# Attention and routed experts on one core: the further tile and its branch ahead of the last expert's down product, two experts' weights in dead tiles, rows fetched on ACT's queue

## The chip, the cores and the metric

The kernel runs on one core of a Trainium2 chip. Its engines are TensorE (PE, with the weight loads shown apart as PEld), VectorE (DVE), ScalarE (ACT), GpSimd (POOL) and SyncE (SP). Each works through its own instructions in the order in which the program gives them. SP, ACT and POOL can start DMA transfers. The metric is the device time of one execution in microseconds (us).

## The reference

A transformer layer with the norms behind the additions: attention with 16 query and 4 key heads, then a layer norm, then eight routed experts of which each token takes one, plus a shared expert, then a second layer norm. All data are 32-bit floats: 2 x 1024 tokens of width 256, experts of inner width 512.

```python
x = L0_attn_x                                             # (2, 1024, 256)
x = _layernorm(x + attn(x, Wq, Wk, Wv, Wo))               # causal, ALiBi, 16 heads, 4 KV heads

logits = x @ router_w.T                                   # 8 experts
top_vals, top_idx = jax.lax.top_k(logits, 1)
scores = sigmoid(where chosen: top_vals, else -inf)
xr = x[None] * scores.T[:, :, None]
gate, up = split(einsum('eth,ehf->etf', xr, gate_up_proj))
routed = einsum('etf,efh->eth', up * silu(gate), down_proj)
shared = (silu(x @ shared_gate_w) * (x @ shared_up_w)) @ shared_down_w
x = _layernorm(x + shared + routed.sum(axis=0))
```

## The kernel before

The program has two stages. The first (lines 262 to 919) does attention for all 16 tiles of 128 tokens, the first norm, the routing, and the shared expert for three of its four blocks of 512 tokens. The second (from line 928) does the rest. The change lies in the second stage. The order of all five engines' work there is the order of the program text (a manual schedule), and waits between engines and DMAs follow from what each instruction reads and writes.

**Slots.** Each expert owns two tiles of 128 slots in the DRAM tensor `slot_x` (`OWN = 2`). A token's row (its 256 numbers, its number `NUM` and its weight `WT`) is scattered to a slot by POOL with an indirect DMA (`scatter_x`, line 250). Tokens beyond an expert's 256 slots go to further tiles, which are made of four quarters of 32 slots, each quarter of one expert (`QU = 4`). `place_more` (line 957) computes the places of these tokens and, for each quarter, the expert it belongs to (`more_e`); the 16 scatters with these second places (`slots2`) follow it, spread over several rounds of the loop. The first further tile is always computed; up to 13 more lie in a conditional block that runs only when more than four quarters are in use.

**One expert.** The steps, each a function of its own, are:

- `load` (940): gate and up weights `wgu` (1 MB) and down weights `wd` (0.5 MB), both on SP's queue. `wgu` has four buffers, `wd` five.
- `fetch` (1079): the expert's rows from `slot_x`, on SP's queue, into one of four `row` buffers.
- `weigh` (1099): DVE multiplies rows by their weights.
- `turn` (1105): TensorE transposes the rows, ACT copies them to `slot_xT`.
- `gate_and_up` (1133): 16 matmuls, which stand in the profile as 32 (each as two), in four groups of eight; two Silu on ACT (1150), two products `slot_h` on DVE (1151). The PSUM tiles of gate and up have two buffers each.
- `down_and_norm` (1154): for each of the two tiles the down product (1158, eight matmuls in the profile), then `norm_and_store` (1114): DVE adds to `zt` (1119), takes statistics (`layernorm`, 224), POOL raises to the power -0.5 (232), DVE normalizes (233), POOL scatters the rows to the output (238).
- `gather_z` (1084): POOL gathers into `zt` what the token has so far (input plus shared expert) from the DRAM tensor `z_dram`.
- For a further tile: `gate_and_up_more` (1171), `turn_h` (1190), `down_and_norm_more` (1198), with the weights of its quarters from `weights_of` (1214), which reads the expert's number at run time.

**The order.** The second stage first loads three experts, does the shared expert for the fourth block (`shared`, `shared_down`; its four results go to `z_dram` on SP's queue at line 1076), fetches rows 0 and 1 and loads expert 3. Then comes the loop over the experts (1236). Round e holds, in this order: the fetch of rows e + 2; the weighting of rows e + 1; gate and up of e; the load of e + 4; one quarter's weights in rounds 1 to 4; the turn of e + 1; down and norm of e - 1; the gathering of z for e + 1; in round 0 `place_more`; two to four of the second scatters. Behind the loop stand the further tile's gate and up, then the last expert's down and norm, then the further tile's down and norm, and at the very end the conditional block: every engine reads the number of quarters in use (line 1269) and branches (line 1275).

Of the kernel before, what the change touches and what calls it, by code (L numbers as in the profile page):

```python
# [9 lines left out]
F32 = mybir.dt.float32  # L10
# [6 lines left out]
P = 128  # L17
# [28 lines left out]
def attn_moe_postln_kernel(  # L46
# [15 lines left out]
    nc = tc.nc  # L62
    B, T, C = x.shape
    E, _, F2 = gate_up.shape
    FF = F2 // 2
    KC = C // P
# [861 lines left out]
    with (  # L928
# [8 lines left out]
        tc.tile_pool(name="rt2", bufs=1) as rtp,  # L937
        tc.manual_schedule(engines=MANUAL),
    ):
        def load(e, tag="", bufs=4):  # L940
            gu = wgup.tile([P, KC, F2], F32, tag=f"wgu{tag}", name="wgu", bufs=bufs)
            d = wgup.tile([P, FC, C], F32, tag=f"wd{tag}", name="wd", bufs=bufs + (bufs > 1))
            if isinstance(e, int):
                e = slice(e, e + 1)
            nc.sync.dma_start(out=gu, in_=gate_up[e].rearrange("e (c p) f -> p (e c) f", p=P))
            nc.sync.dma_start(out=d, in_=down[e].rearrange("e (c p) n -> p (e c) n", p=P))
            return gu, d
# [114 lines left out]
        def shared_down(tb, h):  # L1062
            for i in range(TPB):
                dp = ps_d.tile([P, C], F32, tag="d", name="dp")
                for f in range(FC):
                    nc.tensor.matmul(  # L1066
                        dp,
                        lhsT=h[:, f, ts(i, P)],
                        rhs=sh_d[:, f, :],
                        start=(f == 0),  # L1070
                        stop=(f == FC - 1),
                    )
                tt = tb * TPB + i
                z = actp.tile([P, C], F32, tag="z", name="z")
                nc.vector.tensor_add(z, xs[:, tt, :C], dp)
                nc.sync.dma_start(out=z_dram[ts(tt, P), :], in_=z)


        def fetch(first, n):
            row = slp.tile([P, n, ROW], F32, tag="row", name="row")  # L1080
            nc.sync.dma_start(out=row, in_=slot_xt[:, first : first + n])
            return row

        def gather_z(k, row, n):
            z = zts[k % 4]
            for i in range(n):
                nc.gpsimd.indirect_dma_start(
                    out=z[:, i],
                    out_offset=None,
                    in_=z_dram,  # L1090
                    in_offset=bass.IndirectOffsetOnAxis(
                        ap=row[:, i, NUM : NUM + 1].bitcast(I32), axis=0
                    ),
                    bounds_check=NTT * P - 1,
                    oob_is_err=False,
                )
            return z

        def weigh(row, n):
            for i in range(n):  # L1100
                nc.vector.tensor_scalar_mul(
                    row[:, i, :C], row[:, i, :C], row[:, i, WT : WT + 1]
                )

        def turn(row, n):
            tp = ps_t.tile([P, KC, n, P], F32, tag="t", name="xtp")
            for i in range(n):
                for c in range(KC):
                    nc.tensor.transpose(tp[:, c, i, :], row[:, i, ts(c, P)], ident)
            xT = slp.tile([P, KC, n * P], F32, tag="xT", name="slot_xT", bufs=2)  # L1110
            nc.scalar.copy(xT, tp.rearrange("p c n q -> p c (n q)"))  # L1111
            return xT
# [20 lines left out]
        def gate_and_up(xT, e):  # L1133
            h = hp.tile([P, FC, OWN * P], F32, tag="h", name="slot_h")
            for f in range(0, FC, 2):
                gp = ps_gu.tile([P, 2, OWN * P], F32, tag="g", name="gp")
                up = ps_gu.tile([P, 2, OWN * P], F32, tag="u", name="up")
                for dst, off in ((gp, 0), (up, FF)):
                    for j in range(2):
                        for c in range(KC):  # L1140
                            col = off + (f + j) * P
                            nc.tensor.matmul(  # L1142
                                dst[:, j],
                                lhsT=ws[e][0][:, c, col : col + P],
                                rhs=xT[:, c, :],
                                start=(c == 0),
                                stop=(c == KC - 1),
                            )
                sg = actp.tile([P, 2, OWN * P], F32, tag="sg", name="sg")
                nc.scalar.activation(sg, gp, AF.Silu)  # L1150
                nc.vector.tensor_mul(h[:, f : f + 2], sg, up)
            return h

        def down_and_norm(row, z, h, e):
            def dps(i):
                dp = ps_d.tile([P, C], F32, tag="d", name="dp")
                for f in range(FC):
                    nc.tensor.matmul(  # L1158
                        dp,
                        lhsT=h[:, f, ts(i, P)],  # L1160
                        rhs=ws[e][1][:, f, :],
                        start=(f == 0),
                        stop=(f == FC - 1),
                    )
                return dp

            norm_and_store(row, z, OWN, dps)
# [30 lines left out]
        def down_and_norm_more(row, z, hT, ws):  # L1198
            def dps(i):
                dp = ps_d.tile([P, C], F32, tag="d", name="dp")  # L1200
                for f in range(FC):
                    for k, (_, d_q) in enumerate(ws):
                        nc.tensor.matmul(
                            dp[ts(k, QP)],
                            lhsT=hT[:, f, ts(k, QP)],
                            rhs=d_q[:, f, :],
                            start=(f == 0),
                            stop=(f == FC - 1),
                        )
                return dp  # L1210

            norm_and_store(row, z, 1, dps)

        def weights_of(j, k):

            e = nc.values_load(
                more_e[0:1, j * QU + k : j * QU + k + 1],
                engines=(mybir.EngineType.SP,),
                min_val=0,
                max_val=E - 1,  # L1220
                skip_runtime_bounds_check_because="a count of at most E, bounded by E - 1",
            )
            return load(bass.ds(e, 1), f"{k}", 1)


        ws = {e: load(e) for e in range(3)}
        h = shared(2)
        rows = {e: fetch(e * OWN, OWN) for e in range(2)}
        ws[3] = load(3)
        shared_down(2, h)  # L1230
        weigh(rows[0], OWN)
        zs = {0: gather_z(0, rows[0], OWN)}
        xTs, hTs = {0: turn(rows[0], OWN)}, {}
        again = list(range(NTT))
        quarters = []
        for e in range(E):
            if e + 2 < E:
                rows[e + 2] = fetch((e + 2) * OWN, OWN)
            elif e + 2 == E:
                rows[E] = fetch(E * OWN, 1)  # L1240
            n = OWN if e + 1 < E else 1
            weigh(rows[e + 1], n)
            hTs[e] = gate_and_up(xTs.pop(e), e)
            if e + 4 < E:
                ws[e + 4] = load(e + 4)
            if 0 < e <= QU:
                quarters.append(weights_of(0, e - 1))
            xTs[e + 1] = turn(rows[e + 1], n)
            if e > 0:
                down_and_norm(rows.pop(e - 1), zs.pop(e - 1), hTs.pop(e - 1), e - 1)  # L1250
            zs[e + 1] = gather_z(e + 1, rows[e + 1], n)
            if e == 0:
                place_more()
            k = 4 if e == 0 else 3 if e < 3 else 2
            for tt in again[:k]:
                scatter_x(tt, slots2[:, tt : tt + 1])
            del again[:k]

        def more(k, row, z, xT, ws, before=()):
            h = gate_and_up_more(xT, ws)  # L1260
            for what in before:
                what()
            down_and_norm_more(row, z, turn_h(h), ws)

        def last_own():
            down_and_norm(rows[E - 1], zs[E - 1], hTs.pop(E - 1), E - 1)

        more(E, rows[E], zs[E], xTs.pop(E), quarters, [last_own])
        n = nc.values_load(
            how_many[0:1, 0:1],  # L1270
            min_val=0,
# [3 lines left out]
        with tc.If(n > QU):  # L1275
            for j in range(1, NO):
                quarters = [weights_of(j, k) for k in range(QU)]
                row = fetch(E * OWN + j, 1)
                weigh(row, 1)
                z = gather_z(E + j, row, 1)  # L1280
                more(E + j, row, z, turn(row, 1), quarters)


# [42 lines left out]
```

## Time and profile before

| what | us |
|---|---|
| median of 3 runs (lowest, highest) | 565.85 (565.15, 569.23) |
| the profiled execution, its own time | 567.34 |
| its span, from the first to the last instruction | 565.6 |
| TensorE busy | 538.3 (95% of the span) |
| VectorE busy | 340.0 |
| ScalarE busy | 261.8 |
| GpSimd busy | 153.1 |
| second stage, from about | 430 |

The profile is of one execution. Its page gives the busy time of each engine, the chain of work that ended last, groups of equal instructions with what ended the engine's idle time before them, and the DMA issues with their time to landing. The letter q behind an engine's name (SPq, PEldq, POOLq) marks its sequencer, which waits, branches and issues DMAs; such instructions are not counted as busy time. L1142 is line 1142 of the kernel. `out<-in` gives the tiles that an instruction writes and reads; x8 is a number of instructions. In a row of the time line the first two numbers are the start and the duration, and what ended the idle time before an instruction stands in brackets.

### The profile page before, as it was taken

To read this page: it belongs to the slowest core of one execution; us is meant where nothing else is said; L and a number is where in the kernel's file an instruction comes from. 1 tells how busy PE (TensorE), PEld (TensorE's weight loads), DVE (VectorE), ACT (ScalarE), POOL (GpSimd) and SP (SyncE) were. 2 spreads that over 40 slices of the span, in tenths; PEclk is the share of its full clock that TensorE was granted. 3 is DMA by queue.
4 is the path that set the end of the run, shared out by engine and by line. 5 is a ranking of instruction groups with operands and counts; after the bars stand their busy time and mean duration, and the time that the engine had idled before them with its cause. 6 is when DMAs were issued, how large, how long until landed. Compare 5 with 4: busy or idle time off the path is not lost.

```text
span 565.6 us, 8688 instructions
## 1 busy us (share of the span) xinstructions
PE 538.3 (95%) x3274; PEld 294.5 (52%) x3274; DVE 340.0 (60%) x808; ACT 261.8 (46%) x500; POOL 153.1 (27%) x183
## 2 busy tenths in 40 slices
PE   8999999999999999999999999999999999989990
PEld 4654444543333444434335544544755678878860
DVE  2398977787786777786867864333453245434451
ACT  3432876657666765756586764565111022111110
POOL 5310422201110111020423020142102036756642
PEclk9999999999999999998999999999999999989996
DMA  6212760000000000000100000110138555887210
GB/s 204 41 31 36 222 209 2 2 0 1 2 1 1 1 1 1 2 0 2 48 28 1 1 1 2 37 39 0 39 104 302 177 175 190 298 298 224 84 40 24
DMA packets 27119, 40.61 MB, mean 72 GB/s; under 512 B 3598, under 2 KB 20916, under 8 KB 27072
## 3 DMA queue, kind: packets, MB, share of 16 engines
q1 hardware_dynamic: 23088, 33.27, 18.9%
q0 software_dynamic: 3168, 6.34, 3.3%
q8 instruction: 27, 0.44, 0.3%
q10 hardware_dynamic: 816, 0.39, 0.2%
q14 instruction: 20, 0.16, 0.1%
HBM read 27.70 MB, written 12.58 MB: 71 GB/s over the span
## 4 chain that ended last, share of the span: by engine, by line
PE 76%; issue 8%; DVE 6%; ACT 4%; POOL 2%; DMA 1%; POOLq 0%; ACTq 0%; DVEq 0%
PE t_ps L503 18%; PE s_ps L418 10%; PE yT L547 10%; PE dp L1158 5%; PE gp L1142 4%; PE up L1142 4%; PE gu_sh L706 3%; DVE past L437 3%; PE qpj L292 3%; PE dp_sh L726 2%; PE o_ps L592 2%; PE kpj L292 1%; PE gp L1050 1%; PE vpj L327 1%; PE dp L1066 1%
## 5 line engine op out<-in xcount | busy, mean ns | idle before, releaser
L418 PE MATMUL s_ps<-kT,qT 32*128 32x512 f32 (+2 forms) x896 | 185.2, 472 | 1.8 <-ACT diag L452 0.8
L437 DVE TENSOR_REDUCE past<-s_ps 128x1 f32<-128x512 f32 (+3 forms) x256 | 148.0, 617 | 59.0 <-PE s_ps L418 51.9
L503 PE MATMUL t_ps<-qS,kT 32*128 32x512 f32 x576 | 169.1, 640 | 0.3 <-ACT pD L525 0.3
L522 ACT ACTIVATE pT<-t_ps 128x512 f32<-128x512 f32 x224 | 121.4, 600 | 77.0 <-PE s_ps L418 50.8
L418 PEld LDWEIGHTS s_ps<-kT,qT 32*128 32x128 f32 x896 | 79.6, 185 | 16.7 <-DVE past L437 4.9
L503 PEld LDWEIGHTS t_ps<-qS,kT 32*128 32x128 f32 x576 | 52.3, 184 | 59.5 <-issue 31.2
L547 PE MATMUL yT<-pT,v 128*32 128x512 f32 x448 | 60.4, 611 | 0.0
L232 POOL TENSOR_TENSOR rstd<-rstd,neg_half 128x1 f32<-128x1 f32 x33 | 18.8, 571 | 148.5 <-DVE rstd L231 148.5
L527 POOL TENSOR_SCALAR_AFFINE_SELECT pD<-pD 128x1024 f32<-128x1024 f32 x32 | 34.8, 1094 | 77.7 <-ACT pD L525 77.5
L238 POOL DMA_INDIRECT slot_x<-xs,slots x32 | 32.3, 1008 | 43.8 <-DVE slots L687 28.1
L525 ACT COPY pD<-t_ps 128x512 f32<-128x512 f32 x64 | 34.4, 601 | 20.0 <-PE s_ps L418 14.6
L706 PE MATMUL gu_sh<-x1T,sh_gu 128*128 128x512 f32 x96 | 43.6, 597 | 0.0
L455 POOL TENSOR_SCALAR_AFFINE_SELECT diag<-diag 128x1024 f32<-128x1024 f32 x16 | 17.5, 1094 | 92.3 <-ACT diag L452 92.3
L467 DVE TENSOR_REDUCE past<-diag 128x4 f32<-128x512 f32 x64 | 41.9, 676 | 0.0
L1150 ACT ACTIVATE sg<-gp 128x512 f32<-128x512 f32 x16 | 9.6, 597 | 56.1 <-PE gp L1142 56.1
L539 ACT ACTIVATE pD<-pD 128x1024 f32<-128x1024 f32 x32 | 34.3, 1072 | 0.7 <-POOL pD L527 0.7
L452 ACT COPY diag<-s_ps 128x128 f32<-128x128 f32 (+2 forms) x64 | 23.9, 377 | 22.5 <-DVE past L437 19.9
L1142 PE MATMUL gp<-slot_xT,wgu 128*128 128x256 f32 x128 | 30.5, 381 | 1.2 <-ACT slot_xT L1111 1.2
L1158 PE MATMUL dp<-wd,slot_h 128*128 128x256 f32 x128 | 30.6, 395 | 0.0
L450 DVE TENSOR_TENSOR diag<-s_ps,causal 128x128 f32<-128x128 f32 (+2 forms) x64 | 26.4, 415 | 7.1 <-PE s_ps L418 6.9
L1142 PE MATMUL up<-slot_xT,wgu 128*128 128x256 f32 x128 | 30.2, 379 | 0.0
L547 PEld LDWEIGHTS yT<-pT,v 128*32 128x32 f32 x448 | 8.8, 108 | 35.2 <-issue 34.0
(171 smaller groups left out, 619.4 us busy)
## 6 DMA issues: line engine op xcount, KB each, us to landing
wgu<-_L_ffn_gate_up_proj_dram SPq DMA_DIRECT2D x12, 1024.0 KB, 7.8
wd<-in_L_ffn_down_proj_dram SPq DMA_DIRECT2D x12, 512.0 KB, 6.7
slot_x<-empty SPq DMA_DIRECT2D x1, 3900.0 KB, 17.8
row<-slot_x SPq DMA_DIRECT2D x8, 260.0 KB, 2.8
xs<-in_L_attn_x_dram SPq DMA_DIRECT2D x4, 512.0 KB, 6.8
qT<-q_all SPq DMA_DIRECT2D x32, 64.0 KB, 2.3
z_dram<-z_sh SPq DMA_DIRECT2D x12, 128.0 KB, 1.8
sh_gu<-L_ffn_shared_gate_w_dram SPq DMA_DIRECT2D x1, 512.0 KB, 3.9
```

The source lines that it names most:

```text
L418: lambda r=r: nc.tensor.matmul(sp[:, r * n * P : (r + 1) * n * P], lhsT=qT[b][rows, r0 + r, ts(qt, P)], rhs=kT[b][rows, key * P : (key + n ...
L437: nc.vector.tensor_reduce(past[:, h * HALF + j, heads, parts[b, qt][key]], sp[j][:, :, : past_n * P], AX.X, ALU.max, negate=True,)
L467: lambda g=g: nc.vector.tensor_reduce(past[:, g, :, 0], diag[:, g], AX.X, ALU.max, negate=True),
L503: lambda: nc.tensor.matmul(tp, lhsT=kT[b][rows, ts(kt, P)], rhs=qS[b, qt][rows].rearrange("p r q -> p (r q)"), start=True, stop=True,)
L522: nc.scalar.activation(p[:, j], tp[j], AF.Exp)
L525: nc.scalar.copy(p[:, j], tp[j])
L527: nc.gpsimd.affine_select(out=p, in_=p, pattern=[[0, HALF * REP], [1, P]], compare_op=ALU.is_ge, fill=MASKED, base=0, channel_multiplier=-1,)
L539: lambda: nc.scalar.activation(p, p, AF.Exp),
L547: nc.tensor.matmul(yTs[b, qt][g * PAD : (g + 1) * PAD], lhsT=vs[b][:, kt, g, :], rhs=p[:, g, :], start=start, stop=stop,)
L706: nc.tensor.matmul(gu[k], lhsT=sh_gu[:, c, col : col + P], rhs=x1T[:, c, ts(tb, TB)], start=(c == 0), stop=(c == KC - 1),)
L1142: nc.tensor.matmul(dst[:, j], lhsT=ws[e][0][:, c, col : col + P], rhs=xT[:, c, :], start=(c == 0), stop=(c == KC - 1),)
L1158: nc.tensor.matmul(dp, lhsT=h[:, f, ts(i, P)], rhs=ws[e][1][:, f, :], start=(f == 0), stop=(f == FC - 1),)
```

## The change

- **Rows on ACT's queue.** `fetch` issues on ACT's queue; only rows 0 and 1, which are fetched ahead of the loop, stay on SP's.
- **Dead tiles.** The weights of experts 4 and 5 are loaded ahead of `shared_down`, into tiles whose contents are no longer needed: gate and up into the two halves of `x1T`, down into the two halves of `sh_gu`. Loads 6 and 7 follow in rounds 0 and 1. `wd` has four buffers instead of five.
- **Order.** The list `works` puts the further tile (E) between experts 6 and 7 in the loop: its gate and up come where expert 7's were, and its down product follows expert 7's gate and up. The conditional block stands behind the loop, and the last expert's down and norm behind the conditional block.
- **Second scatters.** Rounds 1 to 4 issue three each (before: 3, 3, 2, 2, 2 in rounds 1 to 5).

```diff
-        def load(e, tag="", bufs=4):
-            gu = wgup.tile([P, KC, F2], F32, tag=f"wgu{tag}", name="wgu", bufs=bufs)
-            d = wgup.tile([P, FC, C], F32, tag=f"wd{tag}", name="wd", bufs=bufs + (bufs > 1))
+        def load(e, tag="", bufs=4, place=None):
+            if place is None:
+                gu = wgup.tile([P, KC, F2], F32, tag=f"wgu{tag}", name="wgu", bufs=bufs)
+                d = wgup.tile([P, FC, C], F32, tag=f"wd{tag}", name="wd", bufs=bufs)
+            else:
+                gu, d = place
...
-        def fetch(first, n):
-            row = slp.tile([P, n, ROW], F32, tag="row", name="row")
-            nc.sync.dma_start(out=row, in_=slot_xt[:, first : first + n])
+        def fetch(first, n, queue=nc.scalar, tag="row", bufs=4):
+
+            row = slp.tile([P, n, ROW], F32, tag=tag, name="row", bufs=bufs)
+            queue.dma_start(out=row, in_=slot_xt[:, first : first + n])
...
         ws = {e: load(e) for e in range(3)}
         h = shared(2)
-        rows = {e: fetch(e * OWN, OWN) for e in range(2)}
+        rows = {e: fetch(e * OWN, OWN, nc.sync) for e in range(2)}
         ws[3] = load(3)
+        for i in range(2):
+
+            d = sh_gu[:, i].rearrange("p (f c) -> p f c", f=FC)
+            ws[4 + i] = load(4 + i, place=(x1T[:, :, ts(i, F2)], d))
         shared_down(2, h)
+        works = [*range(E - 1), E, E - 1]
+        many = {w: OWN if w < E else 1 for w in works}
...
+        begin(0)
+        xTs[0] = turn(rows[0], OWN)
+        for i, w in enumerate(works):
+            if i + 2 < len(works):
+                v = works[i + 2]
+                rows[v] = fetch(v * OWN, many[v])
+            if i + 1 < len(works):
+                weigh(rows[works[i + 1]], many[works[i + 1]])
+            if w < E:
+                hTs[w] = gate_and_up(xTs[w], w)
+            else:
+                h = gate_and_up_more(xTs[w], quarters)
+            if i < 2:
+                ws[6 + i] = load(6 + i)
+            if 0 < i <= QU:
+                quarters.append(weights_of(0, i - 1))
+            if i + 1 < len(works):
+                xTs[works[i + 1]] = turn(rows[works[i + 1]], many[works[i + 1]])
+            if i > 0:
+                down_of(works[i - 1])
+            if w == E:
+                hTs[w] = turn_h(h)
+            if i + 1 < len(works):
+                begin(works[i + 1])
+            if i == 0:
                 place_more()
-            k = 4 if e == 0 else 3 if e < 3 else 2
+            k = 4 if i == 0 else 3
             for tt in again[:k]:
                 scatter_x(tt, slots2[:, tt : tt + 1])
             del again[:k]
...
         with tc.If(n > QU):
             for j in range(1, NO):
...
+        down_of(E - 1)
```

Here `begin(w)` gathers z for w, and `down_of(w)` is `down_and_norm` for an expert and `down_and_norm_more` for the further tile.

More of the change, by code (lines that the diff above doesn't have):

```diff
@@ L1076, in shared_down, with gather_z @@
                 nc.sync.dma_start(out=z_dram[ts(tt, P), :], in_=z)
-        def fetch(first, n):
-            row = slp.tile([P, n, ROW], F32, tag="row", name="row")
-            nc.sync.dma_start(out=row, in_=slot_xt[:, first : first + n])
-            return row
-        def gather_z(k, row, n):
-            z = zts[k % 4]
+        def fetch(first, n, queue=nc.scalar, tag="row", bufs=4):
+            row = slp.tile([P, n, ROW], F32, tag=tag, name="row", bufs=bufs)
+            queue.dma_start(out=row, in_=slot_xt[:, first : first + n])
+            return row
+        def gather_z(z, row, n):
             for i in range(n):
@@ L1227, in attn_moe_postln_kernel @@
         h = shared(2)
-        rows = {e: fetch(e * OWN, OWN) for e in range(2)}
+        rows = {e: fetch(e * OWN, OWN, nc.sync) for e in range(2)}
         ws[3] = load(3)
+        for i in range(2):
+            d = sh_gu[:, i].rearrange("p (f c) -> p f c", f=FC)
+            ws[4 + i] = load(4 + i, place=(x1T[:, :, ts(i, F2)], d))
         shared_down(2, h)
-        weigh(rows[0], OWN)
-        zs = {0: gather_z(0, rows[0], OWN)}
-        xTs, hTs = {0: turn(rows[0], OWN)}, {}
-        again = list(range(NTT))
@@ L1235, in attn_moe_postln_kernel @@
[L1235 to L1252, printed above, removed]
+        works = [*range(E - 1), E, E - 1]
@@ new lines, in attn_moe_postln_kernel, with begin, down_of @@
+        many = {w: OWN if w < E else 1 for w in works}
+        zs, xTs, hTs, quarters = {}, {}, {}, []
+        again = list(range(NTT))
+        def begin(w):
+            zs[w] = gather_z(zts[w % 4], rows[w], many[w])
+        def down_of(w):
+            if w < E:
+                down_and_norm(rows[w], zs[w], hTs[w], w)
+            else:
+                down_and_norm_more(rows[w], zs[w], hTs[w], quarters)
+        weigh(rows[0], OWN)
+        begin(0)
+        xTs[0] = turn(rows[0], OWN)
@@ new lines, in attn_moe_postln_kernel @@
+        for i, w in enumerate(works):
[4 more added lines that the diff above has]
+                weigh(rows[works[i + 1]], many[works[i + 1]])
+            if w < E:
+                hTs[w] = gate_and_up(xTs[w], w)
+            else:
+                h = gate_and_up_more(xTs[w], quarters)
[12 more added lines that the diff above has]
+            if i == 0:
@@ L1257, in attn_moe_postln_kernel @@
             del again[:k]
[L1259 to L1268, printed above, removed]
         n = nc.values_load(
@@ L1277, in attn_moe_postln_kernel @@
                 quarters = [weights_of(j, k) for k in range(QU)]
-                row = fetch(E * OWN + j, 1)
+                row = fetch(E * OWN + j, 1, tag="more_row", bufs=1)
                 weigh(row, 1)
-                z = gather_z(E + j, row, 1)
-                more(E + j, row, z, turn(row, 1), quarters)
+                z = gather_z(zts[1 + j % 2], row, 1)
+                h = gate_and_up_more(turn(row, 1), quarters)
+                down_and_norm_more(row, z, turn_h(h), quarters)
+        down_of(E - 1)
 _INS = [
```

## The prediction

> **What bounds the kernel now.** I read the page first, then the chain of work that ended last from 425 us on, then SP's queue waits, the time line of one round, and the queue rows at the end. The page says that TensorE is the bound.
>
> ```profile
> PE 538.3 (95%) x3274; PEld 294.5 (52%) x3274; DVE 340.0 (60%) x808; ACT 261.8 (46%) x500; POOL 153.1 (27%) x183
> ```
>
> All edits lie behind 437 us. There the chain is matmuls almost throughout, and the gate products of the eight experts (x8 groups at L1142, the further tile at L1177) begin at 453.46, 461.75, 472.81, 483.61, 494.4, 509.23, 520.03, 530.83 and 541.41 us; I call these T0 to T8. An undisturbed round takes 10.8 us. One is longer, T4 to T5:
>
> ```profile
> 499.43 3.57 DMA zt<-z_dram,row
> 503.00 0.35 DVE row L1101
> 503.35 0.04 issue
> 503.39 0.85 PE xtp L1109 x4
> 504.24 4.99 PE dp L1158 x16
> ```
>
> TensorE stands from 500.9 to 503.39 (2.5 us), because the rows of expert 5 came late, and then pays 0.85 + 4.99 us for what takes 0.44 + 3.46 us in the next round: 1.9 us more, at a granted clock of 0.71 from 503.39 to 509.23. So 4.4 us could be won here. Who holds row fetches is in SP's queue waits from 420 us on:
>
> ```profile
> SPq L1081 <- DMA slot_x<-xs,slots: 52.6, 7, 11.1
> SPq L1081 <- DMA out_dram<-zt,row: 10.8, 3, 5.8
> ```
>
> A fetch reads slot_x, so it waits for every scatter into slot_x ahead of it in the program. These waits cost SP 63 us and nobody else much, since SP computes nothing. The round of T2 in the time line shows what that means:
>
> ```profile
> 474.58 0.60 ACT L1150 ACTIVATE sg<-gp 128x512 f32<-128x512 f32 x1 [4.60 <-PE gp L1142]
> ...
> 478.03 0.60 ACT L1150 ACTIVATE sg<-gp 128x512 f32<-128x512 f32 x1 [2.86 <-PE gp L1142]
> ...
> 480.19 0.58 ACT L1111 COPY slot_xT<-xtp 128x512 f32<-128x512 f32 x1 [1.57 <-PE xtp L1109]
> ...
> 483.11 0.97 POOL L238 DMA_INDIRECT slot_x<-xs,slots  x1 [0.30 <-issue]
> ...
> 485.63 0.37 SPq L1081 DMA_DIRECT2D row<-slot_x  x1
> ```
>
> The fetch that stands first in this round is issued at T2 + 12.8 us, 2.5 us after the last scatter was issued; ACT has by then done both Silu and the copy of xT. For rounds 1 to 5 the fetch comes at T + 10.7, 12.8, 16.3, 16.4 and 12.6 us, the Silu at about T + 1.8 and + 5.2.
>
> **Rows on ACT's queue: the large term.** The fetch stays the first instruction of its round, but now on ACT. Queued behind it are Silu one, Silu two and the copy of xT; behind these the two products h on DVE, behind those (DVE's program order) the additions of the down product and its statistics, behind these POOL's powers, output scatters, gathers and slot_x scatters, and the last of these releases the next fetch. What was a wait beside the round becomes a ring. The Trainium skill speaks against this edit ("DMA: Bandwidth & Descriptors", Issuing engines are not separate DMA queues): another issuing engine saves only the sequencer's issue time. By the rule it is worth 0.37 us of SP a fetch (the row above), for the seven fetches that move 2.6 us of a queue that is not the bound; by the row it puts an 11 us wait in front of a Silu. The same page (Anatomy of one DMA) says that the issuing sequencer does the waiting; SP's rows agree. I go by the row.
>
> One turn of the ring, from A (slot scatters landed): waits and issue on ACT 0.65 us (0.5 is what ACT's three issues at the start took), two Silu 1.1, copy 0.6: the next gate product starts at A + 2.4. DVE ends the second h at A + 2.5; addition, two statistics and the small sum take 1.3, twice, to A + 5.1; the power and the normalization bring the first output scatter to A + 6.1. From there POOL issues two outputs, two gathers, three slot scatters: 485.85 to 493.80 in the trace, 7.95 us, so the last is issued at A + 14.1. Landing took 2.4 us (the one of 483.11) and 5.6 to 6.6 us under weight loads (three at 491 to 494). One turn is 16.5 us bare, some 18 to 20 under load, against 10.8. TensorE's round, even with 1.9 us of low clock, fits into it. The change issues 4, 3, 3, 3, 3 slot scatters in rounds 0 to 4 (before 4, 3, 3, 2, 2, 2 in 0 to 5), so the fetches of rounds 1 to 5 wait and every turn has three.
>
> **Two experts in dead tiles: earlier loads, later z.** Loads 4 and 5 (3.15 MB) go out between about 440 and 445 us, ahead of the shared expert's z on the same queue.
>
> ```profile
> 440.00:452.00 12.00, 11.31 (x43) 7.75 (x41) 3.29 (x8) 0.60 (x1) 0.00 (x0) 1.00 0.54 187
> ...
> 446.61 5.50 SPq L1076 DMA_DIRECT2D z_dram<-z  x4
> ```
>
> The columns of the first row end in granted clock, DMA share, GB/s. In steps of 2 us, 440 to 448 moved 1.98 MB. With 3.15 MB more, at 340 GB/s (432 to 434 us), that lasts to 455. The z writes do not overtake: one issued at 429.98 landed after 6.2 us, when the load issued at 427.44 ahead of it (8.2 us) was through; unhindered they take 1.7. So the first z lands near 455.6 instead of 448.3. DVE's third addition needs its buffer, the rows' weighting stands behind the fourth, then turn and copy: 2.7 us from the landing to the first gate product, 458.3 instead of 453.46, +4.8. TensorE stands some 5 us before that, so +1.9 for the clock: the first round ends 6.7 us late, with it the counts, the second places and their scatters. If the loads found free time instead, this is 0; if they held all four z writes in turn, 9. I take 6.7.
>
> **The sum up to T6.** A1 is 472.4 + 6.7 = 479.1. The quarter loads are no longer mixed with fetches; they go out in one run with the last expert's second half, 6.8 MB, once the down product of expert 1 is done (about 494), and last 20 us. So A2 = 479.1 + 14.1 + 4.2 = 497.4 and A3 = 515.7, both with a landing between bare and loaded; A4 = 532.2, A5 = 548.7. T6 = 551.1, 31 us after the 520.03 of before. In it the 4.4 us stall is already gone. The tile wd loses its fifth buffer, so the second halves of loads 6 and 7 wait for the down products of experts 0 and 1 (479 and 494); they are wanted 60 us later: nothing. The fetch of round 6 waits only for output scatters (A5 + 10.3, about T6 + 8); copy and h are done near T6 + 10, before TensorE needs them at T6 + 10.6: nothing.
>
> **Further tile and branch ahead of the last down product.** From T6, TensorE has 6.9 + 0.2 + 3.5 (expert 6 and down of 5), 3.6 + 0.4 + 3.5 + 0.4 (further tile's gates, turn, down of 6, turn of h), 6.9 + 2.1 (expert 7's gates, further tile's down) = 27.5 us, +1.9 of low clock: its end is Y = 580.5. The 0.7 us that TensorE waits before L1203 (549.1 to 549.75) is now covered by expert 7's gates. Then every engine branches:
>
> ```profile
> L1275 PEldq COMPARE_BRANCH x1: 3602/3602/3602, 550.8 to 550.8; - x1
> L1275 POOLq INC_SWDGE_SEM x1: 1508/1508/1508, 557.8 to 557.8; - x1
> L1321 POOLq DRAIN x3: 40/107/5457, 559.3 to 565.4; - x3
> ```
>
> Before, TensorE's 3.6 us lay behind its last matmul. Now 16 matmuls wait for it. Its branch began 1 us before the last matmul of L1203 ended at 551.8 and was over at 554.4, so they start at Y + 2.7. The skill ("Runtime: NRT & Kernel Launch", Instruction fetch mechanics) says that a taken branch leaving the fetched pages stalls for a fetch from memory; it gives no price, the row does. POOL must see its scatters landed (3.0 us for the last), then make up the skipped increments: in before from 551.8 to 559.3, so it is free at Y + 7.5, about when the last statistics come (Y + 7.5 to 9). Powers, two output scatters (second issued at Y + 10.1), landing 3.0, closing 1: Y + 14.2 if the 5.5 us drain goes; Y + 17.4 if a drain follows the last scatter anyway; Y + 19.6 if it is the increment's own work and blocks POOL. I take 17: the trace shows the drain only behind the increment and cannot part them. Before, T6 to the end was 45.6 us; now 29.4 + 17 = 46.4. Without the low clock and with the short close it would be 41.7, a gain of 3.9.
>
> **Sum.** The span goes from 565.6 to 580.5 + 17 = 597.5, +31.9 us. The profiled execution took 567.34, 1.5 us over the 565.85 us median; added to the median the difference gives 597.8, so 598 us.
>
> **Rivals.**
> - *The ring is looser or the start is hidden*, 25%. If POOL's work stays tied to TensorE's round as before, rounds are T + 12.8 + 2.4 instead of 16.5 and the total is 592; if the z writes slip through, 591; with both, 586. For it: 187 GB/s at 440 to 452 leaves room. Against: DVE's order puts h ahead of the additions.
> - *The ring is heavier*, 12%: the two landings taken at 4.2 us are 6 us, and the increment blocks POOL: 598 + 3.6 + 2.6 = 604.
> - *ACT is not held*, 7%: the fetch's wait does not stop the Silu behind it. (It would cost nothing if it ended by T + 1.8, and little by T + 5.2.) Then + 6.7 at the start, - 4.4 for the late rows, - 3.9 at the end: 564, no change, and 558 if the start is hidden too. Against: five fetch times of T + 10.7 or more, and SP, which stands at each.
>
> The forecast has 56%. The range leaves out the last rival and reaches over the first two, with 2 us below 586 and 4 above 604 for the low clock and the close: 584 to 608. About 1% (5.7 us) can be told from no change. Faster by more 4%, within it 3%, slower 93%.
>
> **What would show it.** Fetches on ACT's queue with Silu directly behind them; ACT waiting on slot_x scatters some 10 us a round for five rounds; gate products some 16 to 19 us apart up to T6, 10.7 after; the first one near 458; a low granted clock from 460 to 550; TensorE's branch of 3.6 us ahead of the last down product. I am wrong if Silu runs while a fetch still waits, or if the gate products stay 10.8 us apart.

## The result, and the profile after

The changed kernel takes 602.75 us (median of 4; 600.93 to 603.5) against 567.18 us of the kernel before beside it: a ratio of 1.0622, with a 95% interval of 1.0588 to 1.0656. The forecast was 598 us. The profiled execution spans 600.7 us, 35.1 us more than before, and the page shows the same work on the engines:

```profile
PE 547.0 (91%) x3274; PEld 299.1 (50%) x3274; DVE 338.8 (56%) x808; ACT 260.7 (43%) x500; POOL 152.9 (25%) x183
```

TensorE is busy 8.7 us longer with as many instructions (the clock granted to it was 0.69 from 452 to 463 us and 0.87 from 482 to 520), and the rest is standing still. Its longer waits are in its time line from 440 us on; the bracket gives the idle time ahead of a group and what ended it.

```profile
457.78 1.12 PE L1112 MATMUL xtp<-ident,row 128*128 128x128 f32 x4 [6.61 <-DVE row L1104]
...
482.04 1.99 PE L1145 MATMUL gp<-slot_xT,wgu 128*128 128x256 f32 x8 [1.70 <-ACT slot_xT L1114]
...
501.79 3.78 PE L1145 MATMUL gp<-slot_xT,wgu 128*128 128x256 f32 x8 [8.68 <-ACT slot_xT L1114]
...
519.52 2.85 PE L1145 MATMUL gp<-slot_xT,x1T 128*128 128x256 f32 x8 [4.18 <-ACT slot_xT L1114]
...
535.52 1.99 PE L1145 MATMUL gp<-slot_xT,x1T 128*128 128x256 f32 x8 [3.25 <-ACT slot_xT L1114]
...
551.47 3.55 PE L1145 MATMUL gp<-slot_xT,wgu 128*128 128x256 f32 x8 [4.88 <-ACT slot_xT L1114]
...
584.26 5.38 PE L1161 MATMUL dp<-wd,slot_h 128*128 128x256 f32 x16 [3.57 <-DVEq L1291]
```

Three places: once ahead of the first turn (DVE's rows late), five times ahead of gate products (ACT's copy of xT late, 22.7 us together), once ahead of the last down product (the branch). The waits of ACT between 452 and 566 us name the middle one (us in total, times, longest):

```profile
ACT sg L1153 <- DMA slot_x<-xs,slots: 45.0, 3, 16.2
...
ACT sg L1153 <- issue: 18.2, 1, 18.2
ACT sg L1153 <- PE dp L1161: 11.2, 1, 11.2
```

These are five waits, one for each of the rounds 1 to 5. The profile puts three to the slot scatters, one to no cause, and one to a down product that this Silu does not read; but each of the five ends some 0.5 us behind the issue of a fetch on ACT's queue (at 479.95, 499.70, 517.43, 533.44 and 549.41).

The round that begins with the gate product of 482.04 shows one turn of the ring:

```profile
493.74 0.97 POOL L238 DMA_INDIRECT slot_x<-xs,slots  x1 [0.30 <-issue]
...
499.70 0.37 ACTq L1085 DMA_DIRECT2D row<-slot_x  x1
500.17 1.08 ACT L1153 ACTIVATE sg<-gp 128x512 f32<-128x512 f32 x2 [18.18 <-issue]
500.80 1.29 DVE L1154 TENSOR_TENSOR slot_h<-sg,up 128x512 f32<-128x512 f32 x2 [14.35 <-ACT sg L1153]
501.14 0.59 ACT L1114 COPY slot_xT<-xtp 128x512 f32<-128x512 f32 x1
```

The last slot scatter is issued at 493.74 and lands 5.8 us later. Then the fetch is issued, both Silu run back to back (before, they ran 1.8 and 5.2 us into their round), the copy follows, and the gate product starts at 501.79. The Silu had had their inputs since about 484 and 487.

### The profile page after: what moved, and what is told of

It reads as the page before. It is cut to its first block, busy times and chain, and to the rows that moved or that the text cites. A ratio compares the mean times of both kernels' runs of the same rounds, so it can differ in the third digit from the quotient of the medians.

```text
span 600.7 us, 8680 instructions
## 1 busy us (share of the span) xinstructions
PE 547.0 (91%) x3274; PEld 299.1 (50%) x3274; DVE 338.8 (56%) x808; ACT 260.7 (43%) x500; POOL 152.9 (25%) x183
## 3 DMA queue, kind: packets, MB, share of 16 engines
q1 hardware_dynamic: 21312, 31.54, 16.7%
## 5 line engine op out<-in xcount | busy, mean ns | idle before, releaser
L1154 DVE TENSOR_TENSOR slot_h<-sg,up 128x512 f32<-128x512 f32 x16 | 10.5, 686 | 71.8 <-ACT sg L1153 58.5
L1145 PE MATMUL gp<-slot_xT,wgu 128*128 128x256 f32 x96 | 28.0, 443 | 16.5 <-ACT slot_xT L1114 16.5
L1145 PEld LDWEIGHTS gp<-slot_xT,wgu 128*128 128x128 f32 x96 | 20.9, 224 | 21.5 <-ACT slot_xT L1114 18.2
L1161 PE MATMUL dp<-wd,slot_h 128*128 128x256 f32 x96 | 23.5, 401 | 3.6 <-DVEq L1291 3.6
```

The costliest lines, as they stand in the source:

```text
L1145: nc.tensor.matmul(dst[:, j], lhsT=ws[e][0][:, c, col : col + P], rhs=xT[:, c, :], start=(c == 0), stop=(c == KC - 1),)
```

## Experiments

Eleven kernels ran. Spans are of the profiled executions: before 565.6, changed 600.7.

**The ring: queue, position, and what is waited for.** The first kernel puts the fetches back on SP.

```diff
-        def fetch(first, n, queue=nc.scalar, tag="row", bufs=4):
+        def fetch(first, n, queue=nc.sync, tag="row", bufs=4):
```

> The changed kernel, with all row fetches back on SP's queue, nothing else undone. Ring theory (the fetch's wait on ACT stands in front of the Silu, and each round's slot scatters release the next fetch): the gate products go back to 10.8 to 11.1 us apart from T1 = 469.3 on, so T6 comes near 524 instead of 551.5 and the span is 600.7 - 28 = 573 us (570 to 576). Rival (the loads in dead tiles and the new order cost most, the queue little): over 590 us.

Measured: 580.57 us, ratio to before 1.02 (1.0157 to 1.0243), span 580.6. So 20.1 of the 35.1 us go, not 28. All five waits for xT at T2 to T6 are gone and rounds are 10.8 us apart again, but for one: the first view below is of TensorE's waits. Of its 11.7 us for rows, 6.5 are the wait ahead of the first turn, as in the changed kernel. The other 5.2 are new and, with the low clock behind them, make one round 18.3 us long; this is most of what is missing. Expert 4's fetch was issued at 496.11, as soon as the last slot scatter had landed, but on the same queue behind the second half of load 7 (held up until 493.27) and the first quarter's weights; it landed at 504.81, after 8.7 us. The ring had covered this.

```profile
PE xtp L1112 <- DVE row L1104: 11.7, 2, 6.5
PE dp L1161 <- DVEq L1291: 3.6, 1, 3.6
PE gp L1145 <- ACT slot_xT L1114: 1.2, 2, 0.7
```

The second leaves them on ACT and moves them behind the copy.

```diff
-            if i + 2 < len(works):
-                v = works[i + 2]
-                rows[v] = fetch(v * OWN, many[v])
...
                 xTs[works[i + 1]] = turn(rows[works[i + 1]], many[works[i + 1]])
+            if i + 2 < len(works):
+                v = works[i + 2]
+                rows[v] = fetch(v * OWN, many[v])
```

> The changed kernel, fetches still on ACT's queue, but issued behind the round's two Silu and its copy of xT instead of ahead of them. Ring theory: what counts is what is queued behind the wait; now it is the next round's first Silu, wanted 2 us into that round, about when the slot scatters have landed (10.7 to 16 us after the round's start), so nearly all comes back: 573 to 580 us. Rival (ACT's queue itself is the slow one, for instance its issue or its landing): stays within 5 us of the changed kernel, near 600.

Measured: 583.05 us, 1.0244 (1.0201 to 1.0287), span 582.8, 3 us above what was expected. The queue is the same and 17.9 us come back, so it was the position ahead of the Silu. What is left over are again late rows: TensorE waits 16.7 us in four pieces for them, 6.6 of it ahead of the first turn; one fetch, issued at 510.17, took 7.5 us to land under the quarters' loads.

The third keeps queue and position and takes away what makes the fetch wait: the second scatters go to a tensor of their own.

```diff
-    slot_x = tc.dram_tile([SLOTS, ROW], F32, name="slot_x")
+    slot_x = tc.dram_tile([E * OWN * P, ROW], F32, name="slot_x")
+    slot_y = tc.dram_tile([NO * P, ROW], F32, name="slot_y")
...
-                further, begin, float(QP), float((E - 1) * OWN * P), ALU.mult, ALU.add
+                further, begin, float(QP), float(-OWN * P), ALU.mult, ALU.add
...
-                scatter_x(tt, slots2[:, tt : tt + 1])
+                scatter_y(tt, slots2[:, tt : tt + 1])
...
-            queue.dma_start(out=row, in_=slot_xt[:, first : first + n])
+            queue.dma_start(out=row, in_=slot_xt[:, first : first + n] if first < E * OWN else slot_yt[:, first - E * OWN : first - E * OWN + n])
```

> The changed kernel, fetches on ACT's queue and first in their round, but the second scatters write a DRAM tensor of their own (own slots and further slots apart), so a fetch of an expert's own rows no longer waits for them, only for its row buffer's output scatters. Ring theory: the first wait ends about 6 to 9 us into the round, the copy of xT is done before the matmuls of the round are, T6 falls to 525 to 530, the span to 574 to 580 us. Rival (the wait for the row buffer, or POOL's own load, makes the ring): 590 us or more.

Measured: 584.38 us, 1.0295 (1.024 to 1.035), span 581.3, just above what was expected. ACT's waits tell why:

```profile
ACT sg L1159 <- DMA out_dram<-zt,row: 33.5, 3, 12.3
...
ACT sg L1159 <- DMA slot_y<-xs,slots: 14.4, 1, 14.4
```

The further tile's own rows lie in `slot_y`, so its fetch still waits for every second scatter: 14.4 us on ACT, 4.9 on TensorE. I had overlooked it. The waits for output scatters hold ACT longer in sum but end earlier in the round (9.7 to 11.5 us into it, against 14.4), and cost TensorE 1.3 and 0.6 us there. So a looser ring stays: gate products 12.3, 13.1 and, with the slot scatters, 16.0 us apart. The three kernels agree: only the three together (this queue, this position, these scatters) make turns of 16 to 20 us.

The fourth puts only the fetches of the loop of the kernel before on ACT.

```diff
-        def fetch(first, n):
+        def fetch(first, n, queue=nc.scalar):
             row = slp.tile([P, n, ROW], F32, tag="row", name="row")
-            nc.sync.dma_start(out=row, in_=slot_xt[:, first : first + n])
+            queue.dma_start(out=row, in_=slot_xt[:, first : first + n])
...
-        rows = {e: fetch(e * OWN, OWN) for e in range(2)}
+        rows = {e: fetch(e * OWN, OWN, nc.sync) for e in range(2)}
```

> The kernel before, with the row fetches of the loop on ACT's queue and nothing else of the change. Ring theory: turns of 15 to 18 us in rounds 1 to 6 (slot scatters 4, 3, 3, 2, 2, 2), T7 near 556 instead of 530.8, 2 us of low clock: 592 to 596 us. Rival (the ring needs the changed order or the early loads): under 575 us.

Measured: 594.93 us, 1.0463 (1.042 to 1.0507), span 592.9, as expected: this part alone costs 27.3 us. Six of the seven rounds with a fetch have the same mark: Silu stands 13.1 to 15.2 us behind the fetch's wait. The profile puts four of these waits to slot scatters and two to a down product that ended near by:

```profile
ACT sg L1150 <- DMA slot_x<-xs,slots: 57.7, 4, 15.2
ACT sg L1150 <- PE dp L1158: 26.8, 2, 13.6
```

**The early loads.**

```diff
-        for i in range(2):
-            d = sh_gu[:, i].rearrange("p (f c) -> p f c", f=FC)
-            ws[4 + i] = load(4 + i, place=(x1T[:, :, ts(i, F2)], d))
         shared_down(2, h)
+        for i in range(2):
+            d = sh_gu[:, i].rearrange("p (f c) -> p f c", f=FC)
+            ws[4 + i] = load(4 + i, place=(x1T[:, :, ts(i, F2)], d))
```

> The changed kernel, with the loads of experts 4 and 5 issued behind the shared expert's four z writes instead of ahead of them, in the same dead tiles. Theory (the z writes queue behind 3.1 MB of loads and hold DVE's third addition, so the first gate product comes 6 us late and at a low clock): the wait of 6.6 us ahead of the first turn goes, the first gate product stands near 453.5, the whole shifts by 7.4 us: span near 593 us. Rival (the ring has slack that takes it up, or the loads only move the trouble to the gathers): span over 598 us.

Measured: 595.5 us, 1.0502 (1.0439 to 1.0565), span 593.1, as expected. In the changed kernel the stretch 440 to 452 us and DVE's longest wait there are these (columns as before; the DMA share is 0.99 where it was 0.54):

```profile
440.00:452.00 12.00, 11.18 (x42) 7.61 (x41) 2.22 (x4) 0.60 (x1) 0.00 (x0) 1.00 0.99 354
```

```profile
DVE z L1078 <- DMA z_dram<-z: 8.5, 1, 8.5
```

The first z write, issued at 446.5, took 10.1 us to land; with z first, TensorE waits 0.8 us ahead of the first turn instead of 6.6.

**The conditional block.**

```diff
+        down_of(E - 1)
         n = nc.values_load(
...
-        down_of(E - 1)
```

> The changed kernel, with the last expert's down and norm ahead of the conditional block and the block last, as before. Theory (the branch ahead of the last down product costs TensorE 3.6 us and a low clock for its 16 matmuls, 5.4 us together; at the end it costs the wait for the landing and the increments, 3.6 us less gained): the span falls by 2 to 3 us, to 598. Rival (the block ahead of the last product saves time at the end): the span rises.

Measured: 600.09 us, 1.0578 (1.0521 to 1.0636), span 598.6. The span falls by 2.1 us, as the theory has it. But this is one profile of each, the intervals of the two overlap, and either kernel's spans differ by 2.6 us or more among its runs; so the total does not show the gain, and what follows is read from the two profiles. The wait of 3.6 us ahead of the last down product is gone, and TensorE ends at 584.6 instead of 589.6. In the changed kernel the rows of the block's line are (engine, kind, smallest, median and largest time in ns, first and last start in us):

```profile
L1291 PEldq COMPARE_BRANCH x1: 3406/3406/3406, 579.8 to 579.8; - x1
L1291 POOLq INC_SWDGE_SEM x1: 1468/1468/1468, 586.7 to 586.7; - x1
```

and those of the program's last line:

```profile
L1339 POOLq DRAIN x3: 40/113/7547, 592.3 to 600.4; - x3
```

POOL's power for the last norm starts at 588.43, right behind the statistics that it needs (588.36); the increments were over by 588.2 and held up nothing here. The drain is now behind the last scatter (issued 593.44, 0.97 long) and ends 5.5 us after it. The next kernel leaves the block out of the kernel before (left out: further tiles beyond the first).

> The kernel before without its conditional block (left out: further tiles beyond the first, which these inputs don't use). If the drain of 5.5 us on GpSimd follows its last scatter whatever precedes it, the end comes 5.5 us after that scatter's issue instead of 9.1: span 562 us. If the drain is the increments' own work: 556 to 557 us.

Measured: 564.35 us, 0.9932 (0.9901 to 0.9964), span 562.8. POOL's drain in that kernel:

```profile
L1308 POOLq DRAIN x3: 40/107/6755, 555.2 to 562.5; - x3
```

It starts at 555.2 and ends at 561.9, 5.5 us after the last scatter (555.44, 1.04 long), with no increments in the program. So it belongs to the end of the program. The block costs some 3 us at the end, where POOL waits for the landing and makes the increments; ahead of the last product it costs 5 us of TensorE and saves those 3.

**All three undone, and two versions from it.** Fetches on SP's queue, z first, the block last:

> The changed kernel with three parts undone at once: fetches on SP's queue, loads of experts 4 and 5 behind the z writes, the conditional block last. Left of the change: the dead tiles, four buffers of down weights, the further tile between experts 6 and 7, three scatters a round. If the three costs add: 580.6 of the fetches on SP's queue, less 7.4, less 2.6, is a span of 570 to 571 us, with one wait for late rows of about 5 us left. Rival (a cost that is none of the three): over 575 us; or the rows come in time too, then 563 to 566 us.

Measured: 569.9 us, 1.006 (1.0039 to 1.008), span 567.8. So the three parts make 32.9 of the 35.1 us (one by one 20.1, 7.6 and 2.1; the other 3.1 are how they overlap, or noise). One wait stands above TensorE's own work:

```profile
PE xtp L1112 <- DVE row L1104: 7.1, 2, 6.4
```

Expert 4's rows again: fetched at 485.7, landed at 495.0, behind the second half of load 7 (held up until 482.4 by the four buffers of `wd`) and a quarter. Two edits on top are to take that away, the split tensor of the third kernel and the fifth buffer:

```diff
-                d = wgup.tile([P, FC, C], F32, tag=f"wd{tag}", name="wd", bufs=bufs)
+                d = wgup.tile([P, FC, C], F32, tag=f"wd{tag}", name="wd", bufs=bufs + (bufs > 1))
```

> The version with the three parts undone (fetches on SP's queue, z writes first, the block last), with two edits more: the second scatters write a DRAM tensor of their own, and the down weights have five buffers again, so that a fetch waits neither for second scatters nor behind a held-up load. What is left of the change is the dead tiles and the order. Theory (the one wait of 6.4 us for the rows of expert 4, with its low clock some 8 us, is all that stands above the sum of TensorE's work): span near 560 us, below the kernel before. Rival (fetches now queue behind three quarters' loads, and the rows come late all the same): 566 us or more.

Measured: 562.71 us, 0.9898 (0.9868 to 0.9927), span 560.9: 1% faster than the kernel before. TensorE has no wait over 0.8 us left from 440 us on (which of the two edits does it was not tested):

```profile
PE gp L1151 <- ACT slot_xT L1120: 1.2, 2, 0.7
PE xtp L1118 <- DVE row L1110: 0.8, 1, 0.8
```

The tenth kernel is the split alone on the kernel before:

> The kernel before, with only the DRAM tensor of the slots split in two. Theory: its one wait for late rows (2.5 us and 1.9 us of low clock after it) goes, since the fetch of expert 5's rows waits for output scatters alone: span 561 us. Rival (the fetch comes too late behind the loads anyway): no change.

Measured: 562.51 us, 0.9924 (0.99 to 0.9949), span 560.6, as expected. The intervals of the two overlap: what is left of the change (dead tiles, order) shows no worth of its own here. And the ninth kernel with its fetches on ACT, behind the copy:

> The same as the version with split slots, z writes first, the block last and five buffers, but with the fetches on ACT's queue, behind the round's copy of xT. Theory: the fetches pass the loads on SP's queue, the first Silu of the next round is wanted later than the output scatters land, no wait is left: 559 to 562 us. Rival (the output scatters land late under load, and the Silu behind the fetch waits): 565 us or more.

Measured: 565.96 us, 0.9964 (0.9943 to 0.9985), span 563.8. This is the rival's side in time, by another mechanism than either: the fetch of expert 4 was issued at 482.29, in good time, and took 8.5 us to land beside the loads; TensorE waits 2.1 us for its rows. In the ninth kernel the same fetch, issued at 482.49 on SP's queue, took 2.9 us: there the last three quarters' loads stand behind fetches on the queue. Here nothing holds them back; they were issued from 474 to 485 us, and from 482.3 to 490.8 the DMA engines were busy all the time (DMA share 1.06, 378 GB/s). On ACT's queue the rows share these engines with the loads all the same.

## Why the prediction was right

| step | predicted | measured |
|---|---|---|
| first z lands | 455.6 | 456.6 |
| first gate product T0 | 458.3 | 459.6 |
| fetches of rounds 1 to 5 (A) | 479.1, 497.4, 515.7, 532.2, 548.7 | 479.95, 499.7, 517.4, 533.4, 549.4 |
| T6 | 551.1 | 551.5 |
| end of the further tile's down, Y | 580.5 | 580.7 |
| last down product starts | Y + 2.7 | Y + 3.6 |
| end of the span | Y + 17, 597.5 | Y + 20.0, 600.7 |

**The ring** was right in kind and size. Four turns took 69.5 us for 69.6 predicted. That they agree to 0.1 us is luck: the first turn took 19.75 us for 18.3 (its last scatter landed after 5.8 us where I took 4.2), the second 17.7 for 18.3, and the two bare ones 16.0 each for 16.5. The first four kernels show the cause from four sides. The rule weighed against it (another issuing engine saves only issue time) held: in the eleventh kernel a fetch on ACT's queue took 8.5 us to land beside the loads. But it says nothing of what stands behind the wait; the row, not the rule, gave the price.

**The early loads** were right: 6.7 us predicted, 7.6 when undone. The z writes did wait behind them.

**The close** was mis-sized, by 3.0 of the 3.2 us that the span lies above the sum. The step was "Before, T6 to the end was 45.6 us; now 29.4 + 17". Two terms failed. TensorE's restart was taken from its own branch. In the trace TensorE is released by DVE's branch (584.1), whose statistics for the further tile come first: 0.9 us. And I put the second output scatter at Y + 10.1; it came at Y + 12.7, since the 16 matmuls ran at a low clock (5.4 us for 3.5) and DVE's additions wait for them. The drain is the middle case of the three: it follows the last scatter anyway.

**One step is not shown by the total.** The sentence that the stall of 4.4 us is already gone was true only because the ring covered it. The first and eighth kernels, without the ring, have such a stall of 5.2 and 6.4 us, at expert 4's rows: holding up `wd` on SP's queue (costed at nothing) puts a held-up half load and a quarter right ahead of that fetch once it stands on the same queue, and it then takes 8.7 and 9.3 us to land. The ninth kernel, with five buffers and split slots, has no such stall.

## What to carry to other kernels

Before moving a DMA to another engine's queue, write down what is queued behind its wait there: the transfer gains little, and a wait that cost nothing on an engine that only issues stands ahead of computation on one that computes. If the wait closes a ring through three engines, the loop runs at the ring's time, not at the busiest engine's. It is worth more to ask whether the wait is needed: two kinds of rows in one tensor made every fetch of an expert's own rows wait for scatters that it never reads, and splitting the tensor gained what the moves were unable to.

## What the runs showed of the hardware

- GpSimd's drain at the end took 5.5 us from the end of POOL's last work on, in three kernels: the last indirect scatter (changed kernel, and before without the block) or the increments of the block (before, where it ended 9.1 us after the scatter).
- The branch over the skipped block took TensorE 3.6 us before, 3.4 in the changed kernel and 4.4 in the tenth. SP needed 3.0 us from its branch to its next instruction before, 5.5 in the changed kernel; the other engines at most 0.6.
- How long TensorE stands does not alone decide its clock. In the changed kernel the eight gate matmuls behind a wait of 1.7 or 3.25 us took 1.99 us, as at full clock before the change; behind 4.18, 4.88 and 8.68 us they took 2.85, 3.55 and 3.78. Behind a wait of 2.07 us they took 1.99 us in the fourth kernel and 3.68 in the fifth. Before the change 2.1 us without a matmul were enough for 5.0 us instead of 3.5. The Trainium skill ("TensorE: Matmul & The Clock Gate", Part 1: The HAM clock gate) has a free-running window of some 3.4 us, one of which must pass idle before the clock falls. That the outcome is mixed fits a free-running window, but nothing here shows where the windows lay; that 2.1 us were enough does not fit the page, and the measurement stands.
